# Two stacked attention layers: layer 1 of one batch issued inside the passes of layer 0 of the next batch

## Chip, cores and metric

The kernel runs on one core of a Trainium2 chip, in one launch. The metric is device time in microseconds (us) for the whole program; lower is better. Engines are named as the profile names them: PE (TensorE, matrix multiply, with PEld for its weight loads), DVE (VectorE), ACT (ScalarE), POOL (GpSimd) and SP (SyncE, which here only issues DMAs).

## What is computed

There are 8 batches of 2048 nodes with 256 features, all float32, and one 0/1 adjacency matrix of 2048 x 2048 that all batches share. Two layers follow each other, each with a residual and a layer norm.

```python
# layer 0: 4 heads of 64, softmax taken separately over each chunk of 256 columns
scores = einsum('bhnd,bhjcd->bhnjc', q, kc) / sqrt(64)
scores = where(mask == 0, -10.0, clip(scores, -10.0, 10.0))
ctx = einsum('bhnjc,bhjcd->bhnd', softmax(scores, axis=-1), vc)
out = layernorm(ctx @ Wo.T + bo + x) * gamma + beta
x = layernorm(x + out)
# layer 1: graph attention, 4 heads of 64, softmax over all 2048 columns
Wh = x @ W
e = leaky_relu(s_src[:, :, None, :] + s_dst[:, None, :, :], 0.2)   # -inf where adj == 0
h = elu(einsum('bijh,bjhd->bihd', softmax(e, axis=2), Wh))
x = layernorm(x + h)
```

## The kernel before

**Layer 0.** `project` transposes a block of 512 rows of x and makes its part of `qT`, `kT` (features on partitions) and `vaug` (values with a column of ones, so that the same matmul gives the softmax's sum). `attention0(q, ...)` treats 512 rows (one `q`, four per batch) for two pairs of heads (`hp`) and eight chunks of 256 columns (`c`). I call one triple (q, hp, c) a slot; a batch has 4 x 2 x 8 = 64. In a slot PE makes two tiles of scores `ps` (L259), DVE clips and masks each into `pr` (L266: `max` against a constant, `min` against the mask slab), ACT takes the exponential of each (L274), PE multiplies with the values into `pc`, one per head (L288), ACT copies each to `raw` (L295), DVE takes the reciprocal `rd` of the sums (L297), POOL multiplies (`part`, L301) and adds to the accumulator (`acc`, L303). After eight chunks `acc` is transposed into `qT` (L308, L309).

**Between the layers.** `close0` does the output projection, both layer norms and leaves the result in `x1`; `values1` makes layer 1's values `waug` and the two score vectors `sd`; `factors1` makes the exponentials. The row factor goes out to DRAM (`rowD`) so that it can be loaded back as `srow` on all partitions.

**Layer 1.** `attention1` runs over 4 heads and 16 tiles of 128 columns. For each, DVE makes one tile `e` of 128 x 2048 from `srow`, a per-partition factor and the adjacency bytes `et` (L429), and PE multiplies 16 blocks of it into three PSUM banks `pa` (L434), 6, 5 and 5 blocks to a bank (`BANKS`). At the end of a head the banks are copied out, divided (POOL, `hh`, L453) and put through elu into `x1`; `close1` norms and stores.

**Masks.** In batch 0 `mask_slab` loads 2048 columns of the adjacency at a time, transposes them on PE (`pm`), and writes the clip bounds `slab` (DVE, L183) and the bytes `edge` (ACT, L191), which go to DRAM as `clipD` and `edgeD` for the other batches.

**The order of the work.** Within a layer the code hands pieces of other work to the attention loops as a Python generator called `background`: the closing of the previous 512 rows or of the previous batch into layer 0, half of the next batch's projections into layer 1. Each engine's final order is chosen by a scheduler. PSUM has eight banks: `psA` 2 x 2, `psC` 2, `psM` 2. Layer 1 of a batch uses `psA` and `psC`, which layer 0 also uses; layer 0 of the next batch begins when layer 1 has been issued:

```python
for q in range(NCH):
    ...
    attention0(q, slab, background)
...
gd = factors1(b, sd)
background = chain(*later[2:])
attention1(b, gd, background)
```

Of the kernel before, what the change touches and what calls it, by code (L numbers as in the profile page):

```python
# [22 lines left out]
def adj_resnorm_kernel(  # L23
# [37 lines left out]

    consts = ctx.enter_context(tc.tile_pool(name="consts", bufs=1))
    big = ctx.enter_context(tc.tile_pool(name="big", bufs=1))
    wkp = ctx.enter_context(tc.tile_pool(name="wk", bufs=3))
    slabs = ctx.enter_context(tc.tile_pool(name="slabs", bufs=2))
    edges = ctx.enter_context(tc.tile_pool(name="edges", bufs=4))
# [3 lines left out]
    psC = ctx.enter_context(tc.tile_pool(name="psC", bufs=2, space=bass.MemoryType.PSUM))  # L70
    psM = ctx.enter_context(tc.tile_pool(name="psM", bufs=2, space=bass.MemoryType.PSUM))
# [4 lines left out]
    x1 = big.tile([P, NT, F], F32, tag="x1", name="x1")  # L76
    vaug = big.tile([P, NT, H, D1], F32, tag="vaug", name="vaug")
    waug = big.tile([P, NT, H, D1], F32, tag="waug", name="waug")

    clipD = tc.dram_tile([NCH, P, NT, CH], I8, name="clipD")  # L80
    edgeD = tc.dram_tile([P, NT, N], U8, name="edgeD")
    rowD = tc.dram_tile([B, H, N], F32, name="rowD")

# [20 lines left out]

    wq_sb = weights(wqT, "wq_sb")
    wk_sb = weights(wkT, "wk_sb")
    wv_sb = weights(wvT, "wv_sb")
    wo_sb = weights(woT, "wo_sb")
    bq_sb = column(bq, "bq_sb")
    bk_sb = column(bk, "bk_sb")  # L110
# [5 lines left out]

    w1_sb = consts.tile([P, KC, F + 2 * H], F32, tag="w1_sb", name="w1_sb")
    nc.scalar.dma_start(out=w1_sb[:, :, :F], in_=w1.rearrange("(c p) f -> p c f", p=P))
    for k, a in enumerate((a_src, a_dst)):
        a_sb = small.tile([P, F], F32, tag="hh", name="a_sb")  # L120
        nc.scalar.dma_start(out=a_sb, in_=a.rearrange("h d -> (h d)").partition_broadcast(P))
        for c in range(KC):
            wa = small.tile([P, F], F32, tag="ee", name="wa")
            nc.vector.tensor_mul(wa, w1_sb[:, c, :F], a_sb)
            nc.vector.tensor_reduce(
                w1_sb[:, c, F + k * H : F + (k + 1) * H],
                wa.rearrange("p (h d) -> p h d", h=H),
                AX.X,
                ALU.add,
            )  # L130

# [3 lines left out]

    pb0 = psM.tile([P, CH], F32, tag="psM", name="pb0")
    for c in range(KC):
        nc.tensor.matmul(  # L140
            pb0[:, :F],
            lhsT=bv_sb[:, c : c + 1].to_broadcast([P, P]),
            rhs=wo_sb[:, c, :],
            start=(c == 0),
            stop=(c == KC - 1),
        )
    nc.vector.scalar_tensor_tensor(bo_sb, pb0[:, :F], float(NK), bo_sb, op0=ALU.mult, op1=ALU.add)

    def load_block(b, g, name):
        t = blocks.tile([P, QT, F], F32, tag="xb", name=name)  # L150
        nc.sync.dma_start(
            out=t, in_=x[b, g * CH : (g + 1) * CH, :].rearrange("(t p) f -> p t f", p=P)
        )
        return t

    def transposed(src, name):

        dst = blocks.tile([P, KC, CH], F32, tag="xT", name=name)
        for c in range(KC):
            pt = psM.tile([P, CH], F32, tag="psM", name="pt")  # L160
            for k in range(QT):
                nc.tensor.transpose(
                    pt[:, k * P : (k + 1) * P], src[:, k, c * P : (c + 1) * P], identf
                )
            nc.scalar.copy(dst[:, c, :], pt)
        return dst

    def mask_slab(q):

        slab = slabs.tile([P, NT, CH], I8, tag="slab", name="slab")  # L170
        for u in range(QT):
            t = QT * q + u
            araw = wkp.tile([P, N], I32, tag="wk", name="araw")
            nc.sync.dma_start(out=araw, in_=adj[t * P : (t + 1) * P, :])
            ab = blocks.tile([P, N], BF16, tag="xT", name="ab")
            nc.vector.tensor_scalar(ab, araw, 0, None, ALU.not_equal)
            edge = blocks.tile([P, NT, P], U8, tag="xb", name="edge")
            for g in range(NT // 8):
                pm = psM.tile([P, 8, P], BF16, tag="psM", name="pm")
                for k in range(8):  # L180
                    j = 8 * g + k
                    nc.tensor.transpose(pm[:, k, :], ab[:, j * P : (j + 1) * P], identb)
                nc.vector.tensor_scalar(  # L183
                    slab[:, 8 * g : 8 * g + 8, u * P : (u + 1) * P],
                    pm,
                    2 * CLIP,
                    -CLIP,
                    ALU.mult,
                    ALU.add,
                )  # L190
                nc.scalar.copy(edge[:, 8 * g : 8 * g + 8, :], pm)  # L191
            nc.sync.dma_start(out=edgeD[:, :, t * P : (t + 1) * P], in_=edge)
        nc.sync.dma_start(out=clipD[q], in_=slab)
        return slab

    def load_slab(q):
        slab = slabs.tile([P, NT, CH], I8, tag="slab", name="slab")
        nc.sync.dma_start(out=slab, in_=clipD[q])
        return slab

    def project(b, g):

        xT = transposed(load_block(b, g, "xp"), "xT")
        cols = slice(g * CH, (g + 1) * CH)
        for dst, w, bias in ((qT, wq_sb, bq_sb), (kT, wk_sb, bk_sb)):
            for c in range(KC):
                pp = psM.tile([P, CH], F32, tag="psM", name="pp")
                for kc in range(KC):
                    nc.tensor.matmul(  # L209
                        pp,  # L210
                        lhsT=w[:, kc, c * P : (c + 1) * P],
                        rhs=xT[:, kc, :],
                        start=(kc == 0),
                        stop=(kc == KC - 1),
                    )
                nc.scalar.activation(dst[:, c, cols], pp, AF.Identity, bias=bias[:, c : c + 1])
            yield
        for u in range(QT):
            pv = psM.tile([P, F], F32, tag="psM", name="pv")
            for kc in range(KC):  # L220
                nc.tensor.matmul(  # L221
                    pv,
                    lhsT=xT[:, kc, u * P : (u + 1) * P],
                    rhs=wv_sb[:, kc, :],
                    start=(kc == 0),
                    stop=(kc == KC - 1),
                )
            nc.scalar.copy(vaug[:, QT * g + u, :, :D], pv.rearrange("p (h d) -> p h d", h=H))  # L228
        yield

    def rstd_of(src, n, name):

        mv = small.tile([P, n, 2], F32, tag="mv", name="mv_" + name)
        for k in range(n):
            st = small.tile([P, 6], F32, tag="st", name="st_" + name, bufs=4)
            nc.vector.bn_stats(st, src[:, k, :])
            nc.vector.bn_aggr(mv[:, k, :], st)
        rs = small.tile([P, n], F32, tag="rs", name="rs_" + name)
        nc.vector.tensor_scalar(rs, mv[:, :, 1], EPS, None, ALU.add)
        nc.gpsimd.tensor_tensor(rs, rs, nhalf[:, :n], ALU.pow)  # L240
        return mv, rs

    def attention0(q, slab, background):


        cols = slice(q * CH, (q + 1) * CH)
        for hp in range(HP):
            acc = small.tile([P, QT, 2, D], F32, tag="acc", name="acc")
            accv = acc.rearrange("p t k d -> p k t d")
            probs = {}  # L250

            def scores(c):
                pr = wkp.tile([P, KT, 2, CH], F32, tag="wk", name="pr")
                for u in range(KT):
                    t = KT * c + u
                    ps = psA.tile([P, 2, CH], F32, tag="psA", name="ps")
                    for k in range(2):
                        rows = slice(k * D, (k + 1) * D)
                        nc.tensor.matmul(  # L259
                            ps[:, k, :],  # L260
                            lhsT=kT[rows, hp, t * P : (t + 1) * P],
                            rhs=qT[rows, hp, cols],
                            start=True,
                            stop=True,
                        )
                    nc.vector.scalar_tensor_tensor(  # L266
                        pr[:, u],
                        ps,
                        -CLIP,
                        slab[:, t, :].unsqueeze(1).to_broadcast([P, 2, CH]),  # L270
                        op0=ALU.max,
                        op1=ALU.min,
                    )
                    nc.scalar.activation(pr[:, u], pr[:, u], AF.Exp, scale=0.125)  # L274
                probs[c] = pr

            scores(0)
            for c in range(NK):
                if c + 1 < NK:
                    scores(c + 1)  # L280
                pr = probs.pop(c)
                raw = small.tile([P, 2, QT, D1], F32, tag="raw", name="raw")
# [28 lines left out]
    def close0(b, g):  # L311
# [24 lines left out]
        for k in range(QT):  # L336
# [6 lines left out]
            if k % 2:  # L343
                yield
# [204 lines left out]
```

## Time and profile before

| | |
|---|---|
| median of 3 runs | 4715.54 us (4714.53 to 4717.61) |
| the profiled execution | 4709.07 us |
| its span, first to last instruction | 4707.3 us |
| mean granted PE clock | 0.957 |
| instructions | 157,198 |
| HBM read, written | 249.43 MB, 25.43 MB |

The profiled execution is 6.5 us under the median. A batch repeats every 573 us: layer 0's `pr` of the second batch begins at 695.5 us, that of the third at 1268.6 us. Busy time is the time in which an engine has at least one instruction under way. For one instruction the profile gives a duration; the instruction after it on the same engine often starts a little before the first one's end, so the step from start to start is what an instruction costs when the engine has no gap. A row of the costliest groups gives count, busy time, mean duration and, after the second bar, the idle time of the engine before those instructions with what ended it.

### The profile page before, as it was taken

Reading aid. Unit: us, or ns where it says so; the run is one execution under the profiler, and the core shown is the slowest. Engines: PE = TensorE matmul, PEld = TensorE weight load, DVE = VectorE, ACT = ScalarE, POOL = GpSimd, SP = SyncE. Lnnn points to the kernel's source line nnn. Section 1 sums busy time; section 2 is a strip of 40 time slices with the busy share of each in tenths; the row PEclk is TensorE's granted clock in tenths of the full one; section 3 lists DMA queues with packets and bytes.
Section 4 is the critical chain, followed back from the end, with each engine's and each line's share of the span. In section 5 each row is a group of like instructions: output and inputs, shape, how many; then the busy total and the mean of one; then the engine's idle time right before and its main releaser. Section 6 shows DMA issues by size and latency. Waiting matters only on the chain.

```text
span 4707.3 us, 157198 instructions
## 1 busy us (share of the span) xinstructions
PE 4041.1 (86%) x72740; PEld 2922.3 (62%) x72740; DVE 3132.0 (67%) x4113; ACT 1739.0 (37%) x2881; POOL 1649.2 (35%) x1362
## 2 busy tenths in 40 slices
PE   8888888988899888998889988898888998888966
PEld 5555675657755576565766557655576555765666
DVE  3666596555965579564886638866487654976578
ACT  4554205542155412554125530355313552045500
POOL 1444215442154322443224431345213442135421
PEclk9999999999999999999999999999999999999988
DMA  2222331003300032001420013200231002310023
GB/s 89 60 66 89 98 108 33 15 28 107 101 27 24 24 127 87 15 24 31 129 79 24 20 51 121 63 24 20 66 119 58 20 15 80 117 47 20 2 94 99
DMA packets 173154, 284.95 MB, mean 61 GB/s; under 512 B 45136, under 2 KB 96720, under 8 KB 162256
## 3 DMA queue, kind: packets, MB, share of 16 engines
q1 hardware_dynamic: 169600, 272.94, 18.4%
q8 instruction: 568, 9.31, 0.8%
q10 hardware_dynamic: 2896, 1.97, 0.1%
q14 instruction: 90, 0.74, 0.0%
HBM read 249.43 MB, written 25.43 MB: 58 GB/s over the span
## 4 chain that ended last, share of the span: by engine, by line
PE 38%; DVE 26%; POOL 10%; issue 7%; ACT 6%; DMA 1%; DVEq 0%; POOLq 0%; ACTq 0%; SPq 0%
DVE e L429 11%; PE pc L288 10%; PE ps L259 9%; PE pa L434 8%; DVE pr L266 6%; POOL hh L453 3%; ACT pr L274 3%; PE pp L209 3%; PE pw L366 3%; POOL acc L303 2%; ACT raw L295 2%; POOL part L301 2%; PE pv L221 2%; POOL waug L410 1%; DVE tmp L337 1%
## 5 line engine op out<-in xcount | busy, mean ns | idle before, releaser
L274 ACT ACTIVATE pr<-pr 128x1024 f32<-128x1024 f32 x1024 | 1083.1, 1058 | 1276.1 <-DVE pr L266 1272.3
L266 DVE SCALAR_TENSOR_TENSOR pr<-ps,slab 128x1024 f32<-128x1024 f32 x1024 | 1204.9, 1209 | 185.5 <-PE ps L259 185.3
L288 PEld LDWEIGHTS pc<-vaug,pr 128*64 128x64 f32 x32768 | 1023.1, 140 | 456.0 <-issue 214.4
L429 DVE SCALAR_TENSOR_TENSOR e<-srow,gd,et 128x2048 f32<-128x2048 f32 x512 | 1190.0, 2382 | 149.1 <-PE pa L434 80.3
L259 PE MATMUL ps<-qT,kT 64*128 64x512 f32 x4096 | 1144.9, 636 | 142.3 <-DVE pr L266 142.2
L434 PE MATMUL pa<-waug,e 128*64 128x65 f32 x32768 | 1081.9, 228 | 209.7 <-DVE e L429 156.2
L434 PEld LDWEIGHTS pa<-waug,e 128*64 128x64 f32 x32768 | 1028.0, 142 | 286.3 <-DVE e L429 203.1
L288 PE MATMUL pc<-vaug,pr 128*64 128x65 f32 x32768 | 1101.6, 226 | 42.3 <-ACT raw L295 28.1
L301 POOL TENSOR_TENSOR part<-raw,rd 128x512 f32<-128x512 f32 x448 | 469.9, 1049 | 840.5 <-DVE rd L297 784.9
L259 PEld LDWEIGHTS ps<-qT,kT 64*128 64x128 f32 x4096 | 367.2, 189 | 510.9 <-DVE pr L266 237.6
L453 POOL TENSOR_TENSOR hh<-raw,dn 128x320 f32<-128x320 f32 (+1 forms) x96 | 170.3, 1787 | 1225.4 <-DVE dn L450 782.4
L303 POOL TENSOR_TENSOR acc<-acc,part 128x512 f32<-128x512 f32 x448 | 573.4, 1280 | 34.0
L297 DVE RECIPROCAL rd<-raw 128x8 f32<-128x8 f32 x512 | 103.5, 202 | 711.4 <-ACT raw L295 706.8
L295 ACT COPY raw<-pc 128x260 f32<-128x260 f32 x1024 | 371.0, 362 | 120.7 <-PE pc L288 120.3
L447 ACT COPY raw<-pa 128x325 f32<-128x325 f32 (+1 forms) x96 | 39.2, 444 | 570.9 <-PE pa L434 570.9
L301 POOL TENSOR_TENSOR acc<-raw,rd 128x512 f32<-128x512 f32 x64 | 66.7, 1043 | 440.9 <-DVE rd L297 410.3
L410 POOL TENSOR_TENSOR waug<-waug,ed 128x256 f32<-128x256 f32 x128 | 94.6, 778 | 248.6 <-ACT ed L407 248.6
L366 PE MATMUL pw<-w_sb,x1T 128*128 128x264 f32 x512 | 152.8, 432 | 0.3
L324 PE MATMUL po<-wo_sb,qT 128*128 128x256 f32 x512 | 143.5, 430 | 5.2 <-ACT edge L191 4.0
L456 ACT ACTIVATE ee<-hh 128x320 f32<-128x320 f32 (+1 forms) x96 | 46.8, 488 | 262.3 <-POOL hh L453 262.3
L308 PE MATMUL pt<-identf,acc 128*128 128x128 f32 x256 | 43.5, 294 | 107.2 <-POOL acc L303 107.2
L228 ACT COPY vaug<-pv 128x256 f32<-128x256 f32 x128 | 47.6, 372 | 206.6 <-PE pv L221 206.6
(82 smaller groups left out, 2310.3 us busy)
## 6 DMA issues: line engine op xcount, KB each, us to landing
et<-edgeD SPq DMA_DIRECT2D x512, 256.0 KB, 2.7
srow<-rowD SPq DMA_DIRECT2D x32, 1024.0 KB, 6.5
slab<-clipD SPq DMA_DIRECT2D x28, 1024.0 KB, 4.9
xp<-in_x_dram SPq DMA_DIRECT2D x32, 512.0 KB, 4.0
araw<-in_adj_dram SPq DMA_DIRECT2D x16, 1024.0 KB, 5.3
xg<-in_x_dram SPq DMA_DIRECT2D x32, 512.0 KB, 4.1
out_dram<-o SPq DMA_DIRECT2D x32, 512.0 KB, 3.0
edgeD<-edge SPq DMA_DIRECT2D x16, 256.0 KB, 3.4
```

Of the source, the lines that this page charges most:

```text
L259: nc.tensor.matmul(ps[:, k, :], lhsT=kT[rows, hp, t * P : (t + 1) * P], rhs=qT[rows, hp, cols], start=True, stop=True,)
L266: nc.vector.scalar_tensor_tensor(pr[:, u], ps, -CLIP, slab[:, t, :].unsqueeze(1).to_broadcast([P, 2, CH]), op0=ALU.max, op1=ALU.min,)
L274: nc.scalar.activation(pr[:, u], pr[:, u], AF.Exp, scale=0.125)
L288: nc.tensor.matmul(pc[z * D : (z + 1) * D, i, :], lhsT=pr[:, u, k, i * P + z * D : i * P + (z + 1) * D], rhs=vaug[:, KT * c + u, 2 * hp + ...
L295: nc.scalar.copy(raw[:, k], pc)
L301: nc.gpsimd.tensor_mul(part, raw[:, :, :, :D], rd.to_broadcast([P, 2, QT, D]))
L303: nc.gpsimd.tensor_add(accv, accv, part)
L324: nc.tensor.matmul(po[:, k, :], lhsT=qT[:, c, t * P : (t + 1) * P], rhs=wo_sb[:, c, :], start=(c == 0), stop=(c == KC - 1),)
L366: nc.tensor.matmul(pw[:, : F + 2 * H], lhsT=x1T[:, c, u * P : (u + 1) * P], rhs=w1_sb[:, c, :], start=(c == 0), stop=(c == KC - 1),)
L429: nc.vector.scalar_tensor_tensor(e, srow, gd[:, h, t : t + 1], et, op0=ALU.max, op1=ALU.mult)
L434: nc.tensor.matmul(banks[m][z * D : (z + 1) * D, k * D1 : (k + 1) * D1], lhsT=e[:, i * P + z * D : i * P + (z + 1) * D], rhs=waug[:, t, h, :],
L453: nc.gpsimd.tensor_mul(hh, raw[:, :, :D], dn.to_broadcast([P, n, D]))
```

## The change

Every engine now keeps the order in which the code is written (`manual_schedule`), and the code is written slot by slot:

- Layer 1 becomes the class `Layer1`, a list of 192 smaller tiles per batch. A unit is one bank (6 or 5 blocks of 128 rows) of one head, 12 units of 16 tiles; a tile `e` is 128 x 768 or 128 x 640 instead of 128 x 2048. `make` issues the DVE instruction, `use` the matmuls into one bank of a new pool `psL` (2 banks). Each slot of layer 0 of batch b takes three tiles of layer 1 of batch b - 1. The first batch's slots have none; the last batch's layer 1 runs alone at the end.
- Banks: `psA` 2 x 2, `psC` 1, `psL` 2, `psM` 1. `pr` and `e` have four buffers each in pools of their own; the mask slab is loaded per slot.
- All four projections of the next batch stand between two passes, mixed with the closing of the last 512 rows (`between(..., True)`) and `factors`.
- The mask work is cut into 48 pieces: 12 in the first batch's projections, 36 in its first slots, one each.
- `close1` takes layer 0's result back from a DRAM array `x1D`; for the first six batches it runs in the first nine slots two batches later, for the last two in the closing pass.

```diff
+    def mask_piece(t, m):
+        send()
+        araw = ep.tile([P, WIDE * P], I32, tag="e", name="araw")
+        nc.sync.dma_start(out=araw..., in_=adj[...])
+        nc.vector.tensor_scalar(ab[:, : n * P], araw[:, : n * P], 0, None, ALU.not_equal)
+        ...                     # n transposes into pm, one bank of psL
+        nc.vector.tensor_scalar(clip[:, :n], pm[:, :n], 2 * CLIP, -CLIP, ALU.mult, ALU.add)
+        nc.scalar.copy(edge[:, :n], pm[:, :n])
+        outgoing.append(stores)   # clip and edge to DRAM, issued by the next send()
...
+    def normalize(s):
+        nc.vector.reciprocal(rd, raw[:, :, :, D:D1])
+        nc.gpsimd.tensor_mul(part, raw[:, :, :, :D], rd.to_broadcast([P, 2, QT, D]))
+        if c:
+            nc.gpsimd.tensor_add(accv, accv, part)
...
+        def make(self):                       # class Layer1
+            if j == NT // 2:
+                self.load_row(n + 1)
+            if j % JG == 0:
+                self.load_edge(k // JG + 2)
+            nc.vector.scalar_tensor_tensor(
+                e[:, :w], self.rows[n][:, :w], self.gd[:, h, j : j + 1],
+                self.edge[k // JG][:, j % JG, :w], op0=ALU.max, op1=ALU.mult)
+        def step(self):
+            self.rest(1)                      # one part of the last unit's closing
+            for _ in range(STEP):             # STEP = 3
+                self.make()
+                self.use()
...
+        for s in range(SLOTS):
+            send()
+            if s + 3 < SLOTS:
+                load_slab(s + 3)
+            ...
+            if s + 1 < SLOTS:
+                scores(s + 1)                 # 4 matmuls, 2 DVE pr
+                exps(s + 1, 0)
+            if s:
+                normalize(s - 1)
+            product(s, 0)                     # pc of one head, ACT raw
+            if s + 1 < SLOTS:
+                exps(s + 1, 1)
+            if lower:
+                lower.step()
+            elif masks:
+                mask_piece(*masks.pop(0))
+            product(s, 1)
+            ...                               # one piece of between() or close1()
...
+    for s in range(SLOTS):                    # the closing pass
+        lower.step()
+        send()
+        for piece in ending.get(s, []):       # load, add, norm, finish of one close1
+            piece()
```

On DVE a slot with layer 1 in it is therefore, in this order: two `pr` of the next slot, `rd` of the last slot, three `e`, then the piece of other work. On POOL it is `part` and `acc` of the last slot, then what the pieces bring.

## The prediction

> **What bounds the kernel now.** I read the page's busy times first, then the busy time by stage of the second batch, then the groups, then the order of time.
>
> ```profile
> PE 4041.1 (86%) x72740; PEld 2922.3 (62%) x72740; DVE 3132.0 (67%) x4113; ACT 1739.0 (37%) x2881; POOL 1649.2 (35%) x1362
> ```
> ```profile
> 695.50:1031.00 335.50, 303.85 (x4816) 197.94 (x4816) 212.87 (x364) 179.55 (x286) 161.79 (x137) 0.98 0.08 25
> 1031.00:1092.00 61.00, 45.15 (x154) 27.51 (x151) 13.10 (x44) 18.36 (x37) 15.44 (x19) 0.86 0.19 64
> 1092.00:1268.70 176.70, 153.70 (x4095) 140.01 (x4093) 157.50 (x101) 15.33 (x34) 29.63 (x15) 0.93 0.38 116
> ```
>
> The columns are the length, then the busy us of PE, PEld, DVE, ACT and POOL. Layer 0 takes 335 us (5.2 a slot) and fills PE to 91% and DVE to 63%; layer 1 takes 177 us, DVE 89%, POOL nearly free; 61 us lie between. PE is the fullest engine, and layer 1 gives it its gaps, because one `e` on DVE is longer than its matmuls:
>
> ```profile
> L266 DVE SCALAR_TENSOR_TENSOR pr<-ps,slab 128x1024 f32<-128x1024 f32 x1024 | 1204.9, 1209 | 185.5 <-PE ps L259 185.3
> L429 DVE SCALAR_TENSOR_TENSOR e<-srow,gd,et 128x2048 f32<-128x2048 f32 x512 | 1190.0, 2382 | 149.1 <-PE pa L434 80.3
> L301 POOL TENSOR_TENSOR part<-raw,rd 128x512 f32<-128x512 f32 x448 | 469.9, 1049 | 840.5 <-DVE rd L297 784.9
> L303 POOL TENSOR_TENSOR acc<-acc,part 128x512 f32<-128x512 f32 x448 | 573.4, 1280 | 34.0
> ```
>
> Merging the stages puts `e` beside `part` and `acc`. What that costs shows in two stretches of the order of time (start, length, instruction):
>
> ```profile
> 518.69 6.44 POOL L410 TENSOR_TENSOR waug<-waug,ed 128x256 f32<-128x256 f32 x4
> 519.52 7.76 DVE L429 SCALAR_TENSOR_TENSOR e<-srow,gd,et 128x2048 f32<-128x2048 f32 x3 [8.14 <-DMA srow<-rowD]
> ```
> ```profile
> 1344.63 2.31 DVE L266 SCALAR_TENSOR_TENSOR pr<-ps,slab 128x1024 f32<-128x1024 f32 x2
> 1344.80 1.04 POOL L301 TENSOR_TENSOR part<-raw,rd 128x512 f32<-128x512 f32 x1 [1.58 <-DVE rd L297]
> ```
>
> Three `e` take 7.76 us beside POOL where three steps alone are 6.8 (eight take 18.18 elsewhere), and L410, alone 0.6 long, becomes 2.66: they take strict turns. `pr` beside `part` leaves both at their usual length.
>
> **What the Trainium skill says.** "SBUF — State Buffer", Who interferes with whom: a DVE instruction with two SBUF inputs and a GpSimd instruction that reads SBUF exclude each other for a whole instruction, whichever issues first. The trace agrees: `e` reads `srow` and `et`, `pr` one PSUM and one SBUF operand. "PSUM — Partial Sum Buffer", PSUM bank collisions raise a hardware error: no two engines may read one bank together. Here `edge` (L191) waits 21.7 us in all for `slab` (L183), which reads the same bank. "TensorE: Matmul & The Clock Gate", Part 2, Architectural detail: DVE, ACT and POOL run strictly in order, which the order of time shows throughout.
>
> **The change, part by part.** Durations are steps from start to start.
>
> *A combined slot on PE.* In the dense stretch from 1404.04 us, `ps` takes 1.92 and both `pc` 2.01. Layer 1's 64 matmul instructions per slot take 2.0 (L434's 64 span 2.09 including the overlap). Sum 5.93. Other work in the slots of a batch: output 3.9, context transposes 1.1, x1 transposes 1.1, values 4.4, about 32 for the batch. PE: 64 x 5.93 + 32 = 411 a pass.
>
> *A combined slot on DVE.* Two `pr` 2 x 1.134; `rd` 0.12; three `e`. An `e` of 2048 elements steps 2.263 and an affine step of 256 (L340) 0.396, so an element costs 1.04 ns and 0.13 us is fixed; three smaller tiles average 2048 elements together: 2.133 + 3 x 0.13 = 2.52. Sum 4.91, 314 a pass. Extras per 512 rows: two output adds 1.2, two norms of 1.85, eight affine steps of 0.396, four scalings of 0.323: 9.4, three times in slots: 28. Four `close1`: 12.6. Twelve unit closings at 0.58: 7. Sum 362.
>
> *The turns.* In written order POOL's `part` is released by `rd`, 0.28 after it starts; `e` follows `rd` after 0.12, so `e`, `part`, `e`, `acc`, `e`. A blocked POOL operation holds DVE for its length less 0.14 (L410: 0.48 of 0.62), of which DVE hides some 0.11 of its own start (2.63 a turn against 2.263 + 0.48). `part` costs 1.04 - 0.25 = 0.79, `acc` 1.27 - 0.25 = 1.02: 1.8 a slot. Less eight slots without `acc`: 108 a pass. DVE then needs 470, more than PE's 411, so DVE is the bound, and PE is ahead of it. I add 18 for the x1D load that POOL's first add waits for with `part` behind it (10), other POOL reads that meet two-input DVE work (5) and filling (3): **488 a pass**, 7.6 a slot. Bounds: no turns at all 429 (PE with the same 18); every other POOL read of a batch (bias, beta, residual adds, `hh`, norms: 41) paid too, 529.
>
> *Behind the in-order waits.* PE's second `pc` has one bank and needs ACT's `raw`, behind an exponential, behind `pr`: 1.2 + 1.06 + 0.36, then `pc` 1.0 and half of `ps` 0.96, with semaphores 5.0, under the 6.7 of DVE's slot without extras. That wait is covered by DVE; without the turns it would cost little. SP loads a slab three slots ahead and `et` 2.7 slots ahead; their waits on `e` and buffers are covered.
>
> *Between the passes.* Four projections of 1.1 + 3 x 3.6 = 11.9, output 3.9, transposes 1.1, values 4.4, factors and contexts 1.2, bubbles after transposes 4.5: 63, plus 5 for DVE's end against PE's and the first scores: 68, seven times. POOL's `waug` scaling lies under the last projection. The last time there is no projection; its chain was 41 in this trace (4468.9 to 4510.4): 40.
>
> *First batch.* The first `pr` comes at 80.6 us now and layer 0 ends at 456. A mask piece is a chain, because SP issues the next `araw` after the last piece's stores, which wait for `clip` and `edge`: four issues of 0.36, landing 3.3 (256 KB take 2.7, 512 KB 4.0; a piece has 328 to 393), `ab` 0.6, transposes 0.7, `clip` 0.95, `edge` 0.8, semaphores: 7.8 in a slot, 7.5 in the projections. Start 15 + 12 x 7.5 + 20 for what is left: 125. Slots: 36 x 7.8 = 281; 28 without masks at 4.8 (`ps`, `pr`, exponential, `raw`, second `pc` in turn) 134; other PE work 22: 437. Together 562 against 456.
>
> *End.* The lone layer 1: 64 x 2.52 = 161, unit closings and their turns 13. Six `close1` stand whole in one slot: load 4.0, add 2.4, norm 1.85, power 1.1, scaling 1.3, less the three `e` beside it: 8.7 each, 52. After the last slot unit closing and two more `close1` 19, odds 3: 248. Now it is 197 (4510 to 4707).
>
> *Sum of the span:* 125 + 437 + 7 x 68 + 7 x 488 - 13 (no closing in the first combined pass) + 40 + 248 = **4729**, against 4707. A steady batch falls from 573 to 556, which saves 120; start and end give back 157, less 13. The profiled execution adds 1.8 to its span and lies 6.5 under the median, so the median should be **4738**.
>
> **The rivals.**
>
> *PE becomes the bound.* `part` and `acc` fall under `pr`, where two operands don't collide, and a pass is 429. For it: PE is 86% busy, and POOL has 2.3 us of work in a slot with 2.3 of `pr`. Against it: the written order puts `rd` directly ahead of the `e`, and in the first stretch POOL won every turn. Time: 4738 - 7 x 59 = **4325**, faster. It decides if more than 5 us of a pass's 108 us of turns don't happen.
>
> *POOL's other reads are paid too.* Bias, beta, residual add and `hh` are queued after `acc` and slip into the next `e` or the affine steps: 41 a pass for the 5 taken, 7 x 36: **4990**. For it: L337 has two SBUF inputs and averages 701 ns where its shortest is 467. Against: after the third `e` come one-input operations and 2.3 us of `pr`.
>
> *It doesn't do what it says:* the order is printed by the code, and DVE's list has three `e` between `rd` and `pr`. No chance given.
>
> **How the numbers follow.** A measurement can tell some 0.2% (9 us) from no change. My forecast has 0.62; its own range, from 5 us on a start or an end piece and 12 on a pass, is 4620 to 4860, of which about 0.36 lies under 4706, 0.08 within 9 us of 4715.5 and 0.56 above. PE as bound: 0.18. The other reads: 0.20. Faster: 0.62 x 0.36 + 0.18 = 0.40; same 0.05; slower 0.62 x 0.56 + 0.20 = 0.55. Range 4520 to 4970: it leaves out most of the first rival (0.12) and the top of the second (0.08).
>
> **What would show it.** In the profile after: slots 7.6 us apart; DVE over 95% in the passes, with waits of `e` that no semaphore explains, so the second and third `e` of a slot near 1.7 and 1.9 us where 0.9 would be free; `part` and `acc` near 1.7 and 1.8; PE near 80% there, waiting for ACT's `raw` and behind it for `pr`; mask slots of 7.8; closings of 11 in the last pass. It is wrong if `e` stays at 0.9 beside `part`, if slots are 6.5 apart with PE dense, or if mask slots or the gap between passes are over a fifth off.

## The result and the profile after

The changed kernel takes **4770.48 us** (median of four runs, 4760.87 to 4774.93); the kernel before takes 4715.03 beside it. The ratio is 1.0114, 95% interval 1.0097 to 1.0132: slower by 55 us, or 1.1%, where the prediction had 22 us. The profiled execution has a span of 4765.9 us; the working of the prediction gave 4729.

The busy times of the page come first, then its groups of instructions that answer to those of before (count, busy us, mean ns, and behind the second bar the idle time ahead of them):

```profile
PE 4003.2 (84%) x72740; PEld 2936.4 (62%) x72740; DVE 3949.1 (83%) x4954; ACT 1768.1 (37%) x2953; POOL 1999.1 (42%) x1298
...
L622 DVE SCALAR_TENSOR_TENSOR e<-srow,gd,et 128x640 f32<-128x640 f32 (+1 forms) x1536 | 2099.1, 1421 | 8.0 <-DMA et<-edgeD 8.0
...
L317 DVE SCALAR_TENSOR_TENSOR pr<-ps,slab 128x1024 f32<-128x1024 f32 x1024 | 1203.8, 1215 | 258.1 <-PE ps L306 250.9
L361 POOL TENSOR_TENSOR part<-raw,rd 128x512 f32<-128x512 f32 x448 | 592.6, 1323 | 1594.7 <-DVE rd L354 1304.4
...
L363 POOL TENSOR_TENSOR acc<-acc,part 128x512 f32<-128x512 f32 x448 | 758.7, 1693 | 35.2
```

The work of `pr` has not changed, nor has its length (1209 ns before). `part` went from 1049 to 1323 ns, `acc` from 1280 to 1693, and all `e` together from 1190 us to 2099; the smaller tiles alone bring them to 1360 (the scheduler's version below, where hardly any `e` meets POOL). DVE rose from 67% to 83%.

In the order of time (start, length, instruction; "x3" merges three in a row) a combined slot of the third combined pass looks so:

```profile
1899.46 2.36 DVE L317 SCALAR_TENSOR_TENSOR pr<-ps,slab 128x1024 f32<-128x1024 f32 x2
...
1901.73 0.19 DVE L354 RECIPROCAL rd<-raw 128x8 f32<-128x8 f32 x1
...
1901.84 4.36 DVE L622 SCALAR_TENSOR_TENSOR e<-srow,gd,et 128x768 f32<-128x768 f32 x3
...
1902.07 1.65 POOL L361 TENSOR_TENSOR part<-raw,rd 128x512 f32<-128x512 f32 x1 [3.96 <-DVE rd L354]
...
1903.79 1.73 POOL L363 TENSOR_TENSOR acc<-acc,part 128x512 f32<-128x512 f32 x1
```

`rd` releases `part` while the first `e` is under way, and then the engines take turns: one instruction of DVE, one of POOL, and so on. Three `e` last 4.36 us. In the slots of this pass the first `e` has a median of 0.84 us (640 wide) or 0.97 (768), the second 1.67 or 1.80, the third 1.88 or 2.02.

The busy time by stage (start:end, length, then PE, PEld, DVE, ACT, POOL, with counts; at the end the granted PE clock, the DMA share and GB/s). In order: the third combined pass, the start, the first batch's slots, a gap, the last gap, the lone layer 1.

```profile
1732.10:2222.20 490.10, 428.26 (x8776) 321.91 (x8778) 481.01 (x564) 193.02 (x324) 237.19 (x147) 0.95 0.26 75
...
0.00:116.50 116.50, 64.58 (x236) 37.88 (x236) 20.37 (x34) 27.92 (x37) 1.33 (x10) 0.84 0.42 97
116.50:570.50 454.00, 337.66 (x4836) 220.55 (x4836) 263.43 (x359) 203.62 (x321) 153.77 (x126) 0.91 0.29 69
...
1102.50:1172.80 70.30, 62.14 (x292) 39.44 (x287) 14.33 (x45) 23.30 (x40) 19.90 (x14) 0.95 0.18 61
4454.60:4498.80 44.20, 17.58 (x128) 12.95 (x124) 14.32 (x45) 5.76 (x17) 19.77 (x14) 0.73 0.12 43
4498.80:4765.90 267.10, 167.95 (x4096) 146.48 (x4096) 204.31 (x332) 15.78 (x36) 41.49 (x29) 0.81 0.37 107
```

In the pass DVE is busy 98% of the time and PE 87%: DVE is the bound there. Against the kernel before: up to the end of the first batch's slots the kernel loses 570.5 - 456 = 114; between there and the lone layer 1 it gains, 3928 us (570.5 to 4498.8) against 4054 (456 to 4510), so 126; the end takes 267 against 197 (4510 to 4707), a loss of 70. The sum, 58, is the difference of the two spans (58.6).

### The profile page after: what moved, and what is told of

It is laid out like the page before. It is cut to its first block, busy times and chain, and to the rows that moved or that the text cites. A ratio compares the mean times of both kernels' runs of the same rounds, so it can differ in the third digit from the quotient of the medians.

```text
span 4765.9 us, 160296 instructions
## 1 busy us (share of the span) xinstructions
PE 4003.2 (84%) x72740; PEld 2936.4 (62%) x72740; DVE 3949.1 (83%) x4954; ACT 1768.1 (37%) x2953; POOL 1999.1 (42%) x1298
## 4 chain that ended last, share of the span: by engine, by line
DVE 55%; PE 20%; issue 14%; DMA 5%; ACT 3%; POOL 2%; SPq 1%; DVEq 0%; ACTq 0%; POOLq 0%
DVE e L622 31%; DVE pr L317 13%; PE pc L339 4%; PE ps L306 4%; PE pp L250 3%; DMA araw<-in_adj_dram 3%; PE pa L642 2%; PE po L423 2%; PE pv L266 2%; DVE o L390 1%; DVE rd L354 1%; DMA x1g<-x1D 1%; DVE y L443 1%; PE pw L479 1%; DVE st_a L381 1%
## 5 line engine op out<-in xcount | busy, mean ns | idle before, releaser
L622 DVE SCALAR_TENSOR_TENSOR e<-srow,gd,et 128x640 f32<-128x640 f32 (+1 forms) x1536 | 2099.1, 1421 | 8.0 <-DMA et<-edgeD 8.0
L339 PEld LDWEIGHTS pc<-vaug,pr 128*64 128x64 f32 x32768 | 1086.6, 143 | 887.1 <-ACT raw L346 474.9
L339 PE MATMUL pc<-vaug,pr 128*64 128x65 f32 x32768 | 1221.7, 230 | 436.0 <-ACT raw L346 435.7
L361 POOL TENSOR_TENSOR part<-raw,rd 128x512 f32<-128x512 f32 x448 | 592.6, 1323 | 1594.7 <-DVE rd L354 1304.4
L363 POOL TENSOR_TENSOR acc<-acc,part 128x512 f32<-128x512 f32 x448 | 758.7, 1693 | 35.2
L671 POOL TENSOR_TENSOR hh<-raw,dn 128x320 f32<-128x320 f32 (+1 forms) x96 | 125.5, 1307 | 132.6 <-DVE dn L669 132.6
L250 PE MATMUL pp<-xT,wk_sb 128*128 128x512 f32 x256 | 137.3, 686 | 46.2 <-ACT xT L232 46.2
L704 POOL TENSOR_TENSOR h<-h,x1g 128x1024 f32<-128x1024 f32 x32 | 90.0, 2813 | 198.9 <-DMA x1g<-x1D 197.5
L431 DVE TENSOR_TENSOR y<-po,xg 128x512 f32<-128x512 f32 (+1 forms) x56 | 42.6, 761 | 111.0 <-PE po L423 111.0
L434 POOL TENSOR_TENSOR xg<-xg,beta_sb 128x1024 f32<-128x1024 f32 x32 | 87.9, 2746 | 102.1 <-DVE y L431 102.1
```

Source lines behind the costliest of these rows:

```text
L250: nc.tensor.matmul(pp[:, c, :], lhsT=w[:, kc, c * P : (c + 1) * P], rhs=st["xT"][:, kc, :], start=(kc == 0), stop=(kc == KC - 1),)
L339: nc.tensor.matmul(pc[z * D : (z + 1) * D, i, :], lhsT=probs[s][u][:, k, i * P + z * D : i * P + (z + 1) * D], rhs=vaug[:, KT * c + u, 2 * ...
L361: nc.gpsimd.tensor_mul(part, raw[:, :, :, :D], rd.to_broadcast([P, 2, QT, D]))
L363: nc.gpsimd.tensor_add(accv, accv, part)
L622: nc.vector.scalar_tensor_tensor(e[:, :w], self.rows[n][:, :w], self.gd[:, h, j : j + 1], self.edge[k // JG][:, j % JG, :w], op0=ALU.max, ...
```

## The experiments

My theory after the result: turns of `e` with `part` and `acc` make DVE the bound of the passes; the mask pieces are a chain through SP's loads that makes the first batch long; whole closings in one slot make the end long. The rivals: PE, or the single bank of `pc` with ACT's `raw` behind it, is what a pass costs, whatever POOL does; the start and the end cost what their matmuls cost; or the fixed order as such is the cost.

**rd ahead of pr.** `part` and `acc` are to run beside `pr`, which has one SBUF operand.

```diff
-            if s:
-                normalize(s - 1)          # stood between exps(s + 1, 0) and product(s, 0)
+            if s:
+                normalize(s - 1)          # now ahead of scores(s + 1)
             if s + 1 < SLOTS:
                 scores(s + 1)
                 exps(s + 1, 0)
             product(s, 0)
```

> One line moved: the reciprocal, part and acc of the last slot are issued ahead of the scores of the next, so that POOL works while DVE makes the two pr and not while it makes the three e. Theory (e and POOL's reads take turns, 1.8 us a slot): no e waits for POOL any more, e of 640 elements at 0.84 us in all three places, DVE falls to some 372 us a pass and PE (411 and 18 of waits) bounds it; a pass of 488 us becomes 429, seven times 59: 4770 - 413 = about 4355. Rival (the written order itself, with one psC bank and ACT's copy behind an exponential, sets the slot): nothing moves, 4750 to 4790. Between the two the share of 413 tells how much of a slot the turns are.

Measured: 4523.58 us, ratio to before 0.9594 (0.9578 to 0.961), 247 us under the changed kernel. `part` and `acc` are back at medians of 1.04 and 1.28 us. How much of DVE's time the 192 `e` of one pass took shows in the busy time of that tile alone, first of the changed kernel, then of this one:

```profile
1732.10:2222.20 490.10, 275.45 (x192) 0.95 0.26 75
```
```profile
1653.40:2107.50 454.10, 199.97 (x192) 0.97 0.28 81
```

75 us of `e` went, and 36 of the pass; the kernel gained 247 of the 413 us that the theory expected. So the turns are a cost, as the theory says, but the pass did not fall to PE's floor. Nor did all turns go. The `e` take 200 us where the scheduler's version, further down, has 170, and the long ones that are left overlap POOL's additions of `x1g`, bias and beta, a unit's `hh`, or an `acc` that comes late. The same pass over all engines:

```profile
1653.40:2107.50 454.10, 413.16 (x8717) 312.46 (x8718) 409.81 (x563) 192.72 (x321) 186.53 (x147) 0.97 0.28 81
```

PE 413 and DVE 410 of 454: neither is full. Behind the slots with an older batch's closings, slots that carry norms are 7.3 to 9.4 us apart and plain ones 5.5 to 6.8. My reading is that a long DVE slot isn't made up by a short one, because the code issues scores only one slot ahead; no run tests this alone.

**rd behind the three e.** The same from the other side.

```diff
-            if s:
-                normalize(s - 1)
             product(s, 0)
 ...
             elif masks:
                 mask_piece(*masks.pop(0))
+            if s:
+                normalize(s - 1)
             product(s, 1)
```

> The changed kernel with normalize(s-1), that is DVE's reciprocal rd and POOL's part and acc behind it, written after the slot's three e instead of ahead of them. It moves rd the other way than the run that put it ahead of the next slot's pr; in both, part and acc run beside pr. If the turns of e with part and acc are what the changed kernel pays, it is again near that run: e near 0.9 us in all three places, a pass of 450 to 465 us, about 4530 to 4590 us in all. If that run gained because rd and ACT's raw came earlier in the slot, not because of the turns, this one comes later and gains nothing: 4750 us or more.

Measured: 4551.48 us, ratio 0.9653 (0.9639 to 0.9668). The `e` of one pass, again alone:

```profile
1667.90:2127.50 459.60, 180.35 (x192) 0.97 0.28 80
```

Moving `rd` earlier and moving it later gain nearly the same. What both have in common is that `part` and `acc` no longer stand beside the `e` but, in plain slots, beside `pr`; that the gain came from an earlier `raw` is out. In slots with other work part of the turns only moves: the closings' scalings `o` go from 12.6 us in this pass of the changed kernel to 19.4, so that DVE is busy 413 us in the pass, about as with `rd` ahead.

**A third POOL addition.** If the turns are the cost, a further POOL operation in every slot costs what finds an `e` to take turns with.

```diff
             nc.gpsimd.tensor_add(accv, accv, part)
+            nc.gpsimd.tensor_add(part, accv, part)
```

> A third POOL operation per slot: after acc has been added, part = acc + part into the scratch tile, 1.27 us, which nobody reads. Theory (strict turns with three e): the turns e, part, e, acc, e leave no e for it to block; it runs under the next slot's two pr (2.27 us), so the program grows by 0 to 60 us (0 to 0.15 us a slot, more only where the slot's other work has two SBUF inputs): 4770 to 4830. Rival (any POOL read costs DVE its whole length): 56 slots x 7 passes x 1.02 us = 400 more, about 5170.

Measured: 4996.65 us, ratio 1.0594 (1.0578 to 1.061), 226 us over the changed kernel. Neither number was met. In the trace most plain slots keep their 6.5 us; others, which carry a unit's closing, grow from 6.9 or 7.3 to 7.9, and slots with affine steps from 9.1 to 10.2. In the first kind `dn` or `h` of the closing stands between `rd` and the `e`, so that `part` already blocks the first `e`, `acc` the second and the new addition the third. One such slot of this run:

```profile
2003.96 1.04 POOL L361 TENSOR_TENSOR part<-raw,rd 128x512 f32<-128x512 f32 x1 [4.31 <-DVE dn L669]
2004.00 5.30 DVE L623 SCALAR_TENSOR_TENSOR e<-srow,gd,et 128x640 f32<-128x640 f32 x3
...
2006.89 1.73 POOL L364 TENSOR_TENSOR part<-acc,part 128x512 f32<-128x512 f32 x1
```

In the second kind an affine step `y`, with two SBUF inputs, follows the third `e` and meets the new addition. The seven passes together grow from 3397 us (sum of first `pr` to last `e`) to 3596, the first batch's slots from 454 to 468, where the affine steps and scalings got longer too. By these slots a POOL operation is paid for where it meets such DVE work, and is free under `pr`. My "free behind the third `e`" forgot both kinds.

**Mask loads two pieces ahead.**

```diff
...
     def mask_piece(t, m):
         send()
-        araw = ep.tile([P, WIDE * P], I32, tag="e", name="araw")
-        nc.sync.dma_start(out=araw..., in_=adj[...])
+        mask_load()                       # load of the piece after next
+        araw = araws.pop(0)               # two loads are issued before the first piece
```

> The adjacency columns of a mask piece are loaded two pieces ahead instead of after the last piece's stores. Theory (the first batch is a chain through the DMA): mask slots fall from some 8.2 to the 5.6 of the slots without masks, 36 x 2.6 = 94, and the 12 pieces in the projections from 7 each to the projections' own length, some 40: 4770 - 134 = about 4635. Rival (PE at half clock in its gaps, and ab blocked by POOL, hold the mask slot): -30 at most, 4740.

Measured: 4661.16 us, ratio 0.9881 (0.9866 to 0.9896), 109 under the changed kernel. By stage, the start and the first batch's slots:

```profile
0.00:88.80 88.80, 63.04 (x236) 37.82 (x236) 19.51 (x35) 27.84 (x37) 1.33 (x10) 0.91 0.56 135
88.80:467.40 378.60, 311.77 (x4836) 205.21 (x4836) 247.12 (x359) 202.07 (x321) 154.86 (x126) 0.98 0.33 81
```

The start fell by 28 us and the slots by 75. The wait for the load, hidden behind SP's order, was most of the price of the masks; the mask work itself is all still there. A part of the gain is that `ab` no longer meets POOL: its mean fell from 0.79 to 0.48 us, 15 us over the 48 pieces. PE's granted clock in the slots rose from 0.91 to 0.98.

**Closings spread over four slots each.**

```diff
-        for piece in ending.get(s, []):
-            piece()
+        for k in range(4):
+            if s - k in ending:
+                ending[s - k][k]()        # load, add, norm, finish in successive slots
+    last = [close1(B - 1, g) for g in range(len(early), NCH)]
+    for pieces in last:
+        pieces[0]()                       # both last loads before the last unit's rest
     lower.rest(4)
...
```

> In the closing pass the four parts of a close1 (load, add, norm, finish) stand in four successive slots instead of one, and both last loads are issued before the last unit is closed. Theory (each of the six waits some 10 us in DVE's order for its own load, add and power, and the last load waits for the store ahead of it): six closings cost some 4.5 instead of 10.3, 35 in all, and the end 8: 4770 - 43 = about 4727. Rival (the closing pass is bound by e and by PE anyway, or the closings' adds now take turns with e and give it back): 4755 to 4770.

Measured: 4731.4 us, ratio 1.0032 (1.0019 to 1.0045), 39 under the changed kernel. The end, from the lone layer 1 on, falls from 267 to 229 us.

**The next batch's first transposes ahead of the last unit's rest.** At the end of a pass PE waits for the copy `xT`, which stands in ACT's order behind the elu of the last unit, and that behind POOL.

```diff
...
+        turns[0]()                        # load and transposes of the next projection
+        turns[1]()
         normalize(SLOTS - 1)
         if lower:
             lower.rest(4)
...
-        do(*turns[0:3], group[1])
+        do(turns[2], group[1])
```

> In the changed kernel, between two passes, the load and the transposes of the first projection are issued ahead of the last slot's normalization and the last unit's closing; ACT's copy xT then no longer stands behind an exponential that waits for POOL's hh. Theory (this is what made the gap 70 to 72 us instead of 68): PE's wait for xT of 3.8 falls to 1.3, seven gaps: -15, about 4755. Rival (the chain behind it, output and norms, sets the gap): 4765 to 4775.

Measured: 4741.11 us, ratio 1.005 (1.0036 to 1.0064), 29 under the changed kernel, twice what I expected. The six gaps from the last `e` of a pass to the next `pr` sum to 386 us here and to 420 in the changed kernel; the seven passes are 7 us longer together.

**The four edits together** (rd first, masks ahead, closings spread, transposes first).

> The three edits that gained on their own together (POOL's work under the pr: -247, the adjacency loaded two pieces ahead: -109, the closing parts in successive slots: -39), and the first projection's transposes ahead of the last unit's closing between two passes (some -15). Theory (they act on four different stretches: passes, first batch, end, gaps): the gains add up, 4770 - 410 = about 4360, ratio to before 0.925. Rival (they meet: a shorter pass leaves loads and closings uncovered): 4400 to 4450.

Measured: 4365.41 us, ratio 0.9261 (0.9248 to 0.9273). It lies 405 under the changed kernel; the four alone gave 247 + 109 + 39 + 29 = 424. They lie in different stretches of the time and nearly add up.

**raw ahead of the next exponential** (on top of rd first).

```diff
                 scores(s + 1)
-                exps(s + 1, 0)
             product(s, 0)
             if s + 1 < SLOTS:
+                exps(s + 1, 0)
                 exps(s + 1, 1)
```

> On top of e1_rd_first (4524): ACT copies raw of the first head before the exponentials of the next slot, so that PE's second pc no longer waits for a pr and an exponential. Theory (after e1 a pass is a sum over slots of the longer of PE and DVE, and the 41 us in which PE idles lie in slots that DVE fills): a pass falls by 0 to 4 us, and only the first batch's 28 slots without masks gain, some 0.8 each, 22: 4480 to 4515. Rival (the single psC bank and ACT's order hold the passes): 7 x 25 = 175 less, about 4330.

Measured: 4424.88 us, ratio 0.9386 (0.9373 to 0.9399), 99 under rd first alone. The waits, summed over the run (us in total, times, longest), of the changed kernel, of rd first and of this one:

```profile
PE pc L339 <- ACT raw L346: 435.7, 265, 4.9
```
```profile
PE pc L339 <- ACT raw L346: 283.8, 182, 3.2
```
```profile
PE pc L339 <- ACT raw L346: 77.6, 179, 1.0
```

A pass falls from 454 to 440 us. So the single bank of `pc` with the order on ACT does cost something once the turns are gone: 14 us a pass, beside the 36 that taking the turns away brought. The theory had too little for it and the rival too much. What PE waits for most now is DVE, in the same list of this kernel:

```profile
PE pa L642 <- DVE e L622: 117.6, 62, 11.4
PE ps L306 <- DVE pr L317: 95.9, 145, 5.5
```

**The changed text without the fixed order.** The scheduler orders all five engines again.

```diff
-    ctx.enter_context(tc.manual_schedule(engines={...}))
```

> The changed kernel without the call that fixes the written order, so that the scheduler orders each engine as it did before the change. Theory (the cost is that e stands beside POOL's reads, which any order does that lets rd release part while e are waiting): the pass stays within 5% of 488 us, the program between 4650 and 4900. Rival (the in-order waits of the written order are the cost): over 150 us faster than the changed kernel, under 4620.

Measured: 4343.77 us, ratio 0.9213 (0.9201 to 0.9226). My expectation failed by over 300 us, and the rival, that the written order is the cost, held: without it the changed text is 8% faster than the kernel before. But the order of time says that in the passes it is the same cause, seen from the other side:

```profile
1894.64 2.48 DVE L611 SCALAR_TENSOR_TENSOR e<-srow,gd,et 128x640 f32<-128x640 f32 x3 [0.17 <-PE pa L631]
...
1897.21 0.20 DVE L343 RECIPROCAL rd<-raw 128x8 f32<-128x8 f32 x1
...
1897.56 1.04 POOL L350 TENSOR_TENSOR part<-raw,rd 128x512 f32<-128x512 f32 x1 [4.42 <-DVE rd L343]
...
1898.38 2.36 DVE L306 SCALAR_TENSOR_TENSOR pr<-ps,slab 128x1024 f32<-128x1024 f32 x2 [0.97 <-PE ps L295]
...
1898.68 1.28 POOL L352 TENSOR_TENSOR acc<-acc,part 128x512 f32<-128x512 f32 x1
```

It puts `rd` behind the three `e`, so that `part` and `acc` run beside `pr`; three `e` take 2.48 us instead of 4.36 (here 640 wide, there 768). The `e` of one pass take

```profile
1538.50:1986.70 448.20, 169.50 (x192) 0.96 0.27 76
```

against 275.45, so the turns cost the changed kernel 106 us of DVE a pass. All engines in the pass ahead of that one:

```profile
1025.20:1464.00 438.80, 410.35 (x8706) 311.30 (x8708) 369.00 (x508) 194.91 (x319) 164.17 (x138) 0.97 0.27 74
```

DVE is busy 369 us here and 410 with `rd` ahead, and yet this pass takes 439 us, much as the 440 with `raw` ahead. That speaks against the turns that are left there being what holds a pass above PE's busy time. The scheduler also starts the first `pr` at 73.8 us and ends 205 us after the lone layer 1 begins. Where it is worse than the written order is the gap: 84.4 us from the last `e` to the next `pr` in

```profile
1464.00:1548.40 84.40, 65.14 (x362) 41.83 (x356) 34.02 (x100) 24.73 (x44) 35.80 (x23) 0.93 0.32 101
```

and the waits of PE around its end show why:

```profile
PE ps L295 <- DVE pr L306: 13.1, 1, 13.1
```

DVE does four `e` and parts of the closings of an older batch there, 34 us in the gap where the written order has 14, while the second pair of scores waits for the first `pr`.

**All five edits, written, and the same text under the scheduler.** The first is the four edits with `raw` ahead; the second drops the fixed order from it; the third is the changed kernel without the fixed order and with only the mask loads and the closings edited.

> The four edits together (rd first, masks two ahead, closings spread, first projection ahead of the last unit's rest), which gave 4365 us, plus ACT's raw of a slot ahead of the next slot's exponentials. The swap alone on top of rd first took 99 us (14 a pass). Adding up: about 4270 us (4250 to 4300), passes of 436 to 441 us. If the swap takes away slack that the other edits had already used, 4330 to 4365.

> The same text as the five edits together, but without the fixed order, so that the scheduler orders every engine. The scheduler alone on the changed kernel gave 4344 us with a first batch, an end and passes that already lack the mask chain, the whole closings and the turns. So the edits should bring it little: 4320 to 4350 us, and the written order with five edits (about 4270) should be the faster one by one to two per cent. If the text's order still steers the scheduler, it falls to 4270 too.

> The changed kernel without the fixed order and with the mask loads two ahead and the spread closings only. If the scheduler had already taken these two waits away by itself, 4335 to 4350 us, as the scheduler alone (4344); if the written text still limits its start and its end, 4300 us or less.

Measured: 4265.67 us, ratio 0.9047 (0.9034 to 0.9061); 4347.15, ratio 0.9222 (0.9207 to 0.9238); 4343.89, ratio 0.9219 (0.9205 to 0.9233). The first is the fastest kernel of the study. Its stages, the third combined pass, a gap and the end:

```profile
1518.40:1958.80 440.40, 412.15 (x8717) 307.61 (x8718) 411.06 (x563) 195.82 (x321) 186.51 (x147) 0.99 0.29 84
...
1451.70:1518.40 66.70, 61.62 (x344) 40.47 (x343) 14.37 (x43) 24.40 (x44) 19.93 (x14) 1.00 0.21 64
...
4032.00:4264.00 232.00, 168.21 (x4096) 145.97 (x4096) 211.22 (x332) 15.77 (x36) 49.07 (x30) 0.85 0.43 127
```

Its six gaps sum to 401 us and those of the scheduler's version of the changed text to 504; that is more than the whole 78 us between the two kernels. The scheduler gets nothing from the five edits together, nor from the two alone. Its version of the changed text already lacked the waits that the edits take away: its first batch's slots end at 436 us (457 in the fastest kernel), its passes take 440 (440) and its end 205 (232).

## Why the prediction was right and where it was wrong

**Right: which engine becomes the bound, and by what.** The prediction worked out 108 us of turns for a pass; the `e` of a pass take 106 us more than in the scheduler's version. It said 488 us for a pass; the six full ones took 485.5 to 490.1. Its sums of DVE without turns (362) and of PE (411) are close to the 369 and 410 of the scheduler's pass. It said 1.7 and 1.9 us for the second and third `e`, 1.7 and 1.8 for `part` and `acc`; measured 1.67 to 1.80, 1.88 to 2.02, 1.51 and 1.73 (medians). The 7.6 us a slot hold as the mean only: most plain slots are 6.5 to 7.8 us apart, those with norms 8 to 11. PE was to be near 80% in the passes and was at 87. Three runs carry that the turns are the cause: `rd` ahead and `rd` behind both take most of those with `part` and `acc` away without a change in the amount of work, and the third addition adds to them. What "SBUF — State Buffer", Who interferes with whom, of the Trainium skill says (two SBUF inputs on DVE against a POOL instruction that reads) is what decided the case.

**Right: that it loses in all, and why at the two ends.** A steady batch was to fall by 17 us and fell by 14.3 (the mean of the six full passes, 488.7, and of the six gaps, 70.0, against 573), and start and end gave back more than that.

**The step that failed: the prices of the mask chain, the closings at the end and the gaps.** Start and end were to give back 157 us against a saving of 120, and three terms were priced too low: the first batch's slots by 17 us, the end by 19 and the six gaps by 12. By the terms as the prediction wrote them:

| term | predicted | measured | miss |
|---|---|---|---|
| to the first `pr` | 125 | 116.5 | -8.5 |
| first batch's slots | 437 | 454.0 | +17 |
| first gap | 68 | 67.5 | -0.5 |
| first combined pass | 475 | 464.6 | -10.4 |
| six passes | 2928 | 2932.1 | +4.1 |
| six gaps | 408 | 420.0 | +12 |
| last gap | 40 | 44.2 | +4.2 |
| end | 248 | 267.1 | +19.1 |

They sum to +37, which is 4765.9 - 4729. Each is small beside its term, but the forecast was a difference of 22 us between gains and losses of over 100, so that it caught 22 of 55. That the sum is no further off is in part luck: two terms missed the other way, by 19 together. One of them is a slip: for the first combined pass the prediction took away the work of an older batch's closing (13), but not the 10 us that it had added for that closing's load; the pass came out 24 us shorter than the others.

*The mask slots* were to take 7.8 us and took 8.25 on average, 8.1 where no other work stands in them. The chain named is right, as the run with the loads ahead shows; its parts already sum to 7.8, so that the semaphores it lists got nothing, and its link `ab`, which I put at 0.6, isn't constant. Two mask slots in the order of time of the changed kernel, DVE's line and POOL's:

```profile
203.15 1.33 DVE L195 TENSOR_SCALAR ab<-araw 128x640 bf16<-128x640 int32 x1 [1.54 <-DMA araw<-in_adj_dram]
...
212.40 0.49 DVE L195 TENSOR_SCALAR ab<-araw 128x640 bf16<-128x640 int32 x1 [1.15 <-DMA araw<-in_adj_dram]
```
```profile
202.88 1.26 POOL L363 TENSOR_TENSOR acc<-acc,part 128x512 f32<-128x512 f32 x1
...
212.51 1.51 POOL L363 TENSOR_TENSOR acc<-acc,part 128x512 f32<-128x512 f32 x1
```

The first `ab` came while `acc` was running and took 1.33 us; the second came ahead of `acc`, took 0.49, and `acc` waited instead. The same section of the skill says that a `tensor_scalar` whose operands meet its conditions can use the shared ports too, and that the order of issue decides who blocks; these two slots agree. I had read it for `e` alone. In the slots `ab` has a mean of 0.88 us. The loads landed 3.0 to 5.8 us after their issue, with a median of 3.6, where I took 3.3.

*The end.* A closing was to cost 8.7 us more than a plain slot and costs 10 to 13, 10.7 on average, which is 12 us over the six. The parts that the prediction names give only 8.1, for 10.65 less the 2.52 of three `e`. The loads land after 4.0 to 5.4 us where I took 4.0. From the last `e` to the end it takes 28 us where I had 22; the last load is issued only after the store ahead of it. POOL's own waits there, before two of the last three additions:

```profile
  DMA x1g<-x1D: 20.8, 2
```

*The gaps.* I gave 4.5 us to the bubbles behind transposes. In one gap PE waits 6.4 us for `xT` and 2.3 for the load `xp`; the run with the transposes ahead shows that this order cost 34 us over the six gaps, more than the 12 by which I missed them.

**Wrong: the step that a pass without turns is PE's 429.** The prediction put the first rival there, and said of the wait for ACT's `raw` that "without the turns it would cost little". With `part` and `acc` under `pr` a pass takes 454: 14 us of it are that wait. Of the 28 that still lie between 440 and PE's 412, PE's waits for DVE's `e` and `pr` are 20 in such a pass, in slots in which DVE has more to do than PE. I had summed PE and DVE over the pass and taken the larger; by these waits what counts is the larger in each slot. The rival's 4325 should have been about 4500 (4738 less seven times 34).

**Wrong after the result, not before:** I expected the scheduler to do no better than 4650. I had taken the turns for a property of merged layers. Nearly all of them belong to one place in the written order, and a different order of the same instructions avoids them.

**Open.** Whether a version with the written gaps and the scheduler's start and end (73.8 us to the first `pr` and 205 at the end, against 88 and 232 in the fastest kernel) would bring the further 40 us was not tried. How the 28 us of long slots could be evened out wasn't either; a run that issues scores two slots ahead would show whether my reading of them holds.

## What to carry to other kernels

When two stages are merged, look first at which instructions of DVE and POOL will newly run at the same time, and place POOL's reads beside DVE work with a PSUM operand: here one line moved by a few places was worth 5%. Where the code issues work only one slot ahead, sum the engines by slot and not by pass. Where gains and losses of over 100 us nearly cancel, the smaller terms decide the result, so price the chains at the start and the end with the same care. A fixed order should be compared with the scheduler's on the same text: the differences show which waits the written order brings and which it avoids. Here the scheduler has the shorter start and end, and the best written order the shorter gaps.

## What the hardware showed that I had not expected

- Two DVE instructions with one full-sized SBUF input also take turns with POOL: `ab` (int32 to bf16) took 0.49 us alone and 1.33 beside `acc`; the scaling `y` (L390, f32) has a median of 0.40 and a longest of 1.42.
- The turns go one by one even where DVE has its next `e` ready: in the combined passes of the changed kernel none of the 784 multiplications and additions into `part` and `acc` waits for more than one `e`, and no `e` waits for more than one POOL instruction. With one POOL operation between two `e`, both sides pay.
- `pr`, with one PSUM and one SBUF operand, stayed at 1.21 to 1.22 us on average in every version, with and without POOL beside it.
